# Window attention in a fused layer: sums taken with the values, copies in two buffers, a norm begun earlier

## The chip, the cores and the metric

The kernel runs on one core of one Trainium2 chip. The metric is the device time in microseconds (us) of one execution. Fourteen runs of the kernel before have a median of 957.48 us (954.87 to 962.13). The engines are called PE (TensorE: matmuls; PEld is its weight load), DVE (VectorE), ACT (ScalarE), POOL (GpSimd) and SP (SyncE, which issues most of the DMAs).

## The reference

The input is x of 4 x 128 x 64 x 64 (images, channels, rows, columns). Layer 0 norms each pixel over channels, adds a 3x3 depthwise convolution of that norm to it, cuts the image into windows of 16x16 pixels, and attends in each window over 5x5 neighbours, with 2 branches of 4 heads of 32 channels:

```python
y = _layernorm2d(x, ln_g, ln_b)
y = y + _cpe(y, cpe_w, cpe_b)              # 3x3, per channel
logits = jnp.einsum('nbhdij,nbhdkij->nbhkij', q, k_nb) * scale
attn = jax.nn.softmax(logits, axis=3)      # over the 25 neighbours
o = jnp.einsum('nbhkij,nbhdkij->nbhdij', attn, v_nb)
```

Neighbours outside the window are zeros, so each of them adds exp(0) = 1 to the softmax sum and nothing to the output. The heads' outputs are projected, the two branches added, and x added. Layer 1 treats the pixels as tokens: linear attention with a running sum over them (`_L1_attn_ref`), then a recurrence over all 4096 pixels of an image (`_L1_ffn_ref`).

## The kernel before

**Tiling.** A band is 16 rows of one image; there are 16 bands of 4 windows, 64 windows in all. The main loop (L684) goes window by window. For window i it issues:

- `logits` (L355): four masks and 24 products of 32 rows each, four heads side by side in the array, into four PSUM banks; then four exponentials on ACT (L376), each of 128x512, into `es0` to `es3`.
- `weighted` of the window before, i-1 (L379): the softmax sums `den` as four products of a column block of ones with the exponentials (L385), the values `ops` as 24 products (L397), both with 32 output rows per head, so that four heads work side by side. ACT copies both banks to SBUF (`den` L388, `o_sb` L405). A DMA lays the sums out as `dc`, 128 x 16; DVE adds the count of padded neighbours and inverts (L408 to L412); a DMA puts the result in DRAM (`rd`, L414) and another reads it back, one copy for each of 32 rows (`rden`, L416).
- `scaled` of window i-2 (L422): POOL multiplies `o_sb` by `rden` into the band's `oT` (L425).
- `window_inputs` of window i+1 (L315): the products q, k and v from `y2w`, the convolved pixels; each is copied out of PSUM by ACT (L330, L342). Two DMAs (L344, L345) make the middle block of keys out of halves of the two others.

**Gaps.** Between these pieces lie six gaps (`between`, L677). Each gap advances two generators by one step: `behind`, the layer-1 work of the band before (`layer1`, L593: 24 steps, begun in the second window of the next band), and `ahead`, which makes the pixels of the next band (`front`, L646: `norm_rows`, then `convolve` for each half). In the first window of a band `ahead` gets three gaps only (0, 4 and 5), otherwise six: 21 steps in a band. A half of the convolution is one ACT instruction and eight DVE instructions of 128x512 (L271, L273) and a copy to `y2w` on ACT (L309). In the layer-1 order, `output0` (L442) reads `oT` and gives the projected tokens, `measure`, `norm` and `turn` are the second layer norm, `keep` sends tokens to DRAM.

**Order.** `in_order` (L160) keeps PE, DVE, ACT and POOL in the program's order. SP isn't in that list: the order of its DMAs is chosen when the program is built. `p1`, `p2` and `p3` are pools of one, two and three buffers; PSUM is one pool of eight banks, handed out in turn (`bank`, L176). After the main loop a recurrence of 32 steps (L796 on) follows, which the change doesn't touch.

Names of the windows in what follows: a band's **first, second, third and fourth window** are those with i % 4 = 0, 1, 2, 3.

Of the kernel before, what the change touches and what calls it, by code (L numbers as in the profile page):

```python
# [46 lines left out]
def conv_attn_hybrid(ctx: ExitStack, tc: tile.TileContext, ins: dict, out: bass.AP):  # L47
# [101 lines left out]
    for i in range(2):  # L149
        t = const.tile([P, 4, P + 1], F32, name=f"v1_{i}")  # L150
        nc.vector.memset(t, 1.0)
        v1s.append(t)

    stats = const.tile([P, B * T // 512, 6], F32, name="stats")

    wx = const.tile([P, B, NH, SEG, HSEGS], F32, name="wx")
# [22 lines left out]
    def run(g):  # L179
        for _ in g:  # L180
            pass
# [42 lines left out]
    def norm_rows(n):  # L224

        b, wi = bands[n]
        y = padded(n)
        below = wi < NB - 1
        first, end = (0 if wi == 0 else 1), NCH + below

        def evict(dst, src):
            nc.scalar.activation(dst, src, AF.Identity, bias=ln_b, scale=ln_g)

        groups = [(0, 4), (4, 8), (8, 9)] if wi == 0 else [(1, 5), (5, end)]

        found, xn = {}, {}
        for g in range(len(groups) + 2):
            if g < len(groups):
                found[g] = measured(
                    [xin[n][:, j, :] if j < NCH else heads.pop(n + 1) for j in range(*groups[g])],  # L240
                    1e-6,
                )
            if g - 1 in found:
                xn[g - 1] = normed(found.pop(g - 1), p2, "xf")
            if g - 2 in xn:
                j0, j1 = groups[g - 2]
                rows = turned(xn.pop(g - 2), 0, j1 - j0)[:, : (j1 - j0) * P]
                rows = rows.rearrange("p (r w) -> p r w", w=W)
                k1 = min(2 * j1 + 1, WS + 2)
                evict(y[:, 2 * j0 + 1 : k1, 1 : W + 1], rows[:, : k1 - 2 * j0 - 1, :])  # L250
                if j1 > NCH:
                    evict(padded(n + 1)[:, 1:3, 1 : W + 1], rows[:, 2 * (NCH - j0) :, :])
            yield
        ks = slice(1, WS + 1 + below)
        nc.gpsimd.tensor_copy(y[:, ks, 0:1], y[:, ks, 1:2])
        nc.gpsimd.tensor_copy(y[:, ks, W + 1 :], y[:, ks, W : W + 1])

        if wi == 0:
            nc.gpsimd.tensor_copy(y[:, 0, :], y[:, 1, :])
        if below:  # L260
            nc.gpsimd.tensor_copy(padded(n + 1)[:, 0, :], y[:, WS, :])
        else:
            nc.gpsimd.tensor_copy(y[:, WS + 1, :], y[:, WS, :])
# [51 lines left out]
    def window_inputs(w, n, wj):  # L315
# [14 lines left out]
            nc.scalar.copy(w[name], pps)  # L330
            yield
        vps = bank()
        v_sb = p2.tile([P, 3, BR * P], F32, tag="v_sb", name="v_sb")
        for e in range(2):
            nc.tensor.matmul(  # L335
                vps[:, e * 256 : (e + 1) * 256],
# [2 lines left out]
                start=True,  # L339
                stop=True,  # L340
            )
        nc.scalar.copy(v_sb[:, 0::2, :], vps.rearrange("p (e t) -> p e t", e=2))  # L342

        nc.sync.dma_start(v_sb[:64, 1, :], v_sb[64:, 0, :])  # L344
        nc.sync.dma_start(v_sb[64:, 1, :], v_sb[:64, 2, :])  # L345
        w["v"] = v_sb
        yield

    pieces = [(br, n) for br in range(BR) for n in range(len(BLOCKS))]
# [5 lines left out]
    def logits(w):  # L355
# [16 lines left out]
                    stop=(br, n) == pieces[-1],  # L372
                )
        for h in range(HEADS):
            es = p2.tile([P, BR * WT], F32, tag=f"es{h}", name=f"es{h}")
            nc.scalar.activation(es, sps[h], AF.Exp, scale=scale)  # L376
            w["es", h] = es

    def weighted(w):  # L379


        ops, dps = bank(), bank()
        for h in range(HEADS):
            rows = slice(h * HD, (h + 1) * HD)
            nc.tensor.matmul(dps[rows], ones[:, :HD], w["es", h], start=True, stop=True)  # L385

        den = p1.tile([P, BR * WT], F32, tag="den", name="den")
        nc.scalar.copy(den, dps)  # L388
        dc = p2.tile([P, 16], F32, tag="dc", name="dc")
        nc.sync.dma_start(dc, den[::HD, :])  # L390
        yield
        for br, n in pieces:
            cols, _ = spans(br, n)
            for h in range(HEADS):
                rows = slice(h * HD, (h + 1) * HD)
                c0 = br * P + h * HD
                nc.tensor.matmul(  # L397
                    ops[rows, cols],
                    w["v"][:, n, c0 : c0 + HD],
                    w["es", h][:, cols],  # L400
                    start=(br, n) == pieces[0],
                    stop=(br, n) == pieces[-1],
                )
        o_sb = p1.tile([P, BR * WT], F32, tag="o_sb", name="o_sb")
        nc.scalar.copy(o_sb, ops)  # L405
        yield

        nc.vector.tensor_tensor(dc, dc, pad_c, ALU.add)  # L408
        rc = p2.tile([P, 16], F32, tag="rc", name="rc")
        nc.vector.reciprocal(rc, dc)  # L410
        nc.vector.tensor_tensor(dmax, dmax, dc, ALU.max)
        nc.vector.tensor_tensor(dmin, dmin, dc, ALU.min)  # L412
        rd = dram4.tile([HEADS, BR * WT], F32, tag="rd", name="rd")
        nc.sync.dma_start(rd.rearrange("h (a e) -> (h a) e", e=16), rc)  # L414
        rden = p1.tile([P, BR * WT], F32, tag="rden", name="rden")
        nc.sync.dma_start(rden, rd.unsqueeze(1).to_broadcast([HEADS, HD, BR * WT]))  # L416
        w["o"], w["rden"] = o_sb, rden
        yield

# [173 lines left out]
    def layer1(n, last):  # L593
# [2 lines left out]
        y, z = last  # L596
        order = [
            (keep, z), None,
            (norm, z), (product, y), None,
            (output0, a), (measure, a), None,  # L600
            (turn_last, z), None,
            (norm, a), (output0, c), (measure, c), None,
            (turn, a), None,
            (product, z), (norm, c), None,
            (queries, a), None,
# [40 lines left out]
    def front():  # L646


        for n in range(1, len(bands)):
            yield from norm_rows(n)  # L650
            if bands[n][1]:
                yield
            for half in range(2):
                yield from convolve(n, half)
                yield
            if n == 1:

                for _ in range(4):
                    yield


    nc.vector.tensor_scalar(cpe_w[:, 4:5], cpe_w[:, 4:5], 1.0, None, ALU.add)
# [9 lines left out]
    windows = {0: {}}  # L672
    run(window_inputs(windows[0], 0, 0))
    run(third)
    ahead, behind = front(), iter(())

    def between(i, gap):  # L677


        next(behind, None)  # L680
        if i < len(places) and (i == 0 or i % NB or gap in (0, 4, 5)):
            next(ahead, None)

    for i in range(len(places) + 2):  # L684
# [5 lines left out]
        if 2 <= i:  # L690
            m, wjm = places[i - 2]
            if wjm == NB - 1:
                run(behind)
                behind = layer1(m, halves.pop(m - 1, (None, None)))
        between(i, 0)
        if 2 <= i:
            scaled(m, wjm, windows.pop(i - 2))
        if i < len(places) and wj == 1 and n + 2 < len(bands):
            load(n + 2)
        sums = weighted(windows[i - 1]) if 1 <= i <= len(places) else iter(())  # L700
        for gap in (1, 2):
            next(sums, None)
            between(i, gap)
        run(sums)
        if i == 0:
            run(fourth)
        inputs = iter(())
        if i + 1 < len(places):
            windows[i + 1] = {}
            inputs = window_inputs(windows[i + 1], *places[i + 1])  # L710
        for gap in (3, 4, 5):
            next(inputs, None)
            between(i, gap)
        run(inputs)
    run(behind)
    run(layer1_end(*halves.pop(len(bands) - 1)))
    in_order()
# [782 lines left out]
```

## Time and profile before

| | us |
|---|---|
| median of 14 runs | 957.48 |
| the profiled execution's own time | 961.6 |
| its span, first to last instruction | 959.6 |
| PE busy | 884.9 (92%) |
| DVE busy | 747.8 (78%) |
| ACT busy | 542.3 (57%) |
| POOL busy | 263.5 (27%) |
| mean granted clock of PE | 0.972 |
| DMA, share of 16 engines, main queue | 19.1% |

Busy time is the time in which at least one instruction of the engine runs. A group's line gives its line in the kernel, engine and operation, what it writes and reads, its shape and count; then its busy time, the mean of one instruction in ns, and how long the engine was idle just before such an instruction, with what ended that idle time. Matmuls are pipelined and their ends are modelled, so starts of consecutive ones tell more than their lengths. A wait's line reads: who waited for whom, in total, how often, the longest. The span's sum is made against 959.6 us and the profiled time of 961.6, some 4 us above the median of the runs; a change in us is carried over to the median.

### The profile page before, as it was taken

The page shows a single profiled execution, that of the slowest core. Times are in us where ns is not written, and L with a number is a line of the kernel's source. Part 1 is how long each engine was busy: PE and PEld are TensorE (multiplying, and loading weights), DVE is VectorE, ACT ScalarE, POOL GpSimd, SP SyncE. Part 2 cuts the span into 40 slices and gives each one's busy share as a digit, 9 for nine tenths or more (in the row PEclk, how much of TensorE's full clock was granted, in tenths as well). Part 3 has the DMA queues.
Part 4 walks back from the last instruction along what each step waited for, and adds up shares of the span by engine and source line. Part 5 has one row for each costly group of instructions (what it writes and reads, how often), then busy time and mean ns, then how long its engine had stood idle before and what let it go on. Part 6 is the DMA issues. An engine that isn't in the chain of part 4 may idle for free.

```text
span 959.6 us, 26560 instructions
## 1 busy us (share of the span) xinstructions
PE 884.9 (92%) x10508; PEld 657.7 (69%) x10508; DVE 747.8 (78%) x2452; ACT 542.3 (57%) x1010; POOL 263.5 (27%) x359
## 2 busy tenths in 40 slices
PE   5979999999999999999999999999999999978784
PEld 3746676777777768677777767776767778655442
DVE  6345878888887878797888889787879887567786
ACT  3554656575656565665656565656556565522553
POOL 2013131413232231413131323223131312121185
PEclk9978999999999999999999999999999999988898
DMA  3112112121212111212112121111121111101853
GB/s 117 33 36 60 36 52 62 46 57 61 58 46 62 54 55 48 71 37 70 48 45 58 58 57 58 51 57 54 48 66 39 50 40 51 42 34 31 348 203 146
DMA packets 53045, 63.46 MB, mean 66 GB/s; under 512 B 22960, under 2 KB 33840, under 8 KB 52400
## 3 DMA queue, kind: packets, MB, share of 16 engines
q1 hardware_dynamic: 51184, 56.91, 19.1%
q10 hardware_dynamic: 1728, 4.77, 1.3%
q8 instruction: 85, 1.39, 0.6%
q14 instruction: 48, 0.39, 0.2%
HBM read 35.44 MB, written 17.30 MB: 55 GB/s over the span
## 4 chain that ended last, share of the span: by engine, by line
PE 70%; DMA 11%; DVE 7%; ACT 4%; POOL 4%; issue 2%; SPq 1%; ACTq 0%; POOLq 0%; DVEq 0%
PE bank L322 10%; PE bank L450 6%; PE bank L367 6%; DMA rden<-rd 6%; PE bank L212 6%; PE bank L397 5%; PE bank L385 5%; PE bank L335 5%; PE bank L479 5%; PE bank L558 3%; PE bank L587 3%; PE bank L539 3%; PE bank L522 3%; PE bank L560 3%; DMA res<-resd 2%; PE bank L496 2%
## 5 line engine op out<-in xcount | busy, mean ns | idle before, releaser
L273 DVE SCALAR_TENSOR_TENSOR y<-ypad,cpe_w,y 128x512 f32<-128x512 f32 x240 | 191.4, 798 | 14.2 <-ACT y L271 10.6
L425 POOL TENSOR_TENSOR oT<-o_sb,rden 128x512 f32<-128x512 f32 x64 | 85.6, 1337 | 365.0 <-DMA rden<-rd 311.1
L376 ACT ACTIVATE es<-bank 128x512 f32<-128x512 f32 x256 | 132.2, 602 | 76.2 <-PE bank L367 76.2
L196 POOL TENSOR_TENSOR rs<-rs,mhalf 128x4 f32<-128x4 f32 (+2 forms) x100 | 107.1, 1071 | 8.3
L367 PEld LDWEIGHTS bank<-q,k 32*128 32x128 f32 x3072 | 98.1, 189 | 9.7 <-ACT k L330 8.7
L367 PE MATMUL bank<-q,k 32*128 32x96 f32 (+1 forms) x3072 | 96.7, 271 | 7.8 <-ACT k L330 7.8
L195 POOL TENSOR_SCALAR rs<-mv 128x4 f32<-128x4 f32 (+2 forms) x100 | 25.1, 251 | 268.9 <-DVE mv L193 174.2
L203 DVE TENSOR_SCALAR xn<-x,mv,rs 128x128 f32<-128x128 f32 x256 | 81.2, 378 | 21.5 <-POOL rs L196 21.5
L405 ACT COPY o_sb<-bank 128x512 f32<-128x512 f32 x64 | 37.6, 587 | 75.0 <-POOL oT L425 57.1
L397 PEld LDWEIGHTS bank<-es,v_sb 128*32 128x32 f32 x3072 | 57.0, 110 | 30.9 <-issue 16.7
L450 PE MATMUL bank<-woT,oT 128*128 128x128 f32 x512 | 67.7, 288 | 5.1 <-POOL oT L425 5.1
L385 PE MATMUL bank<-es,ones 128*32 128x512 f32 x512 | 72.3, 639 | 0.0
L479 PE MATMUL bank<-xl,awT 128*128 128x512 f32 x128 | 70.1, 631 | 1.0 <-ACT xl L474 1.0
L450 PEld LDWEIGHTS bank<-woT,oT 128*128 128x128 f32 x512 | 64.4, 201 | 9.0 <-POOL oT L425 6.2
L397 PE MATMUL bank<-es,v_sb 128*32 128x96 f32 (+1 forms) x3072 | 70.2, 240 | 0.0
L322 PE MATMUL bank<-y2w,wqT 128*128 128x256 f32 x256 | 67.3, 386 | 1.0 <-DVE y2w L273 1.0
L322 PE MATMUL bank<-y2w,wkT 128*128 128x256 f32 x256 | 66.7, 384 | 0.0
L335 PE MATMUL bank<-wvT,y2w 128*128 128x256 f32 x256 | 66.4, 382 | 0.0
L342 ACT COPY v_sb<-bank 128x512 f32<-128x512 f32 x64 | 37.6, 588 | 50.3 <-PE bank L335 49.4
L330 ACT COPY q<-bank 128x512 f32<-128x512 f32 x64 | 37.8, 591 | 39.7 <-PE bank L322 39.3
L191 DVE BATCH_NORM_STATS2 st<-x 128x6 f32<-128x128 f32 x256 | 55.5, 279 | 1.1
L322 PEld LDWEIGHTS bank<-y2w,wqT 128*128 128x128 f32 x256 | 45.6, 193 | 13.0 <-issue 7.2
(124 smaller groups left out, 1734.8 us busy)
## 6 DMA issues: line engine op xcount, KB each, us to landing
rden<-rd SPq DMA_DIRECT2D x64, 256.0 KB
v_sb<-v_sb SPq DMA_DIRECT2D x128, 64.0 KB
resd<-rs_o SPq DMA_DIRECT2D x32, 256.0 KB
out<-ot SPq DMA_DIRECT2D x32, 256.0 KB
xin<-in_xt SPq DMA_DIRECT2D x15, 512.0 KB
res<-resd SPq DMA_DIRECT2D x2, 2048.0 KB
res<-resd ACTq DMA_DIRECT2D x2, 2048.0 KB
dc<-den SPq DMA_DIRECT2D x64, 8.0 KB
```

The costliest lines, as they stand in the source:

```text
L196: nc.gpsimd.tensor_tensor(rs[:, :n], rs[:, :n], mhalf[:, :n], ALU.pow)
L203: nc.vector.tensor_scalar(xn[:, j, :], piece, mv[:, j, 0:1], rs[:, j : j + 1], ALU.subtract, ALU.mult)
L273: nc.vector.scalar_tensor_tensor(y2, src, cpe_w[:, tap : tap + 1], y2, ALU.mult, ALU.add)
L322: nc.tensor.matmul(pps[:, br * WT : (br + 1) * WT], wT[:, br * P : (br + 1) * P], y2, start=True, stop=True,)
L335: nc.tensor.matmul(vps[:, e * 256 : (e + 1) * 256], y2[:, e * P : (e + 1) * P], wvT, start=True, stop=True,)
L367: nc.tensor.matmul(sps[h][:, cols], w["k"][rows, k0 : k0 + P], w["q"][rows, cols], start=False, stop=(br, n) == pieces[-1],)
L376: nc.scalar.activation(es, sps[h], AF.Exp, scale=scale)
L385: nc.tensor.matmul(dps[rows], ones[:, :HD], w["es", h], start=True, stop=True)
L397: nc.tensor.matmul(ops[rows, cols], w["v"][:, n, c0 : c0 + HD], w["es", h][:, cols], start=(br, n) == pieces[0], stop=(br, n) == pieces[-1],)
L425: nc.gpsimd.tensor_tensor(oTs[n][:, :, :, wj * WS : (wj + 1) * WS], w["o"].rearrange("p (a r c) -> p a r c", a=BR, c=WS), w["rden"].rearra ...
L450: nc.tensor.matmul(yps[:, j * P : (j + 1) * P], oT[:, br, t], woT[:, br, :], start=br == 0, stop=br == BR - 1,)
L479: nc.tensor.matmul(zps, awT[:, m * P : (m + 1) * P], h.xl, start=True, stop=True)
```

## The change

1. **Copied attention in two buffers.** `o_sb` moves from `p1` to `p2`; the exponentials `es0` to `es3` move from `p2` to `p1`; `den` goes away, `o_mid` (one buffer) comes.
2. **Order of the window.** `weighted` of window i now runs in window i itself, its two matmul parts ahead of gaps 3 and 4, and its last part (the inverse and its DMAs) after the next window's logits. `window_inputs` of i+1 moves forward: q ahead of gap 1, k ahead of gap 2, v ahead of gap 5 rather than ahead of gaps 3, 4 and 5. `scaled` runs for window i-1 ahead of v.
3. **Norm of the band ahead.** `norm_rows` is cut into single steps (measure, measure, scale, then turn with the next scale), and `ahead` gets the gaps 0, 2 and 4 of a band's first window. The empty steps are counted anew, so that the convolution keeps its place. In `layer1` the order of the first steps changes: `output0` and `measure` of the first half come second rather than third, and those of the other half fourth rather than fifth; `norm` of the first half then follows `measure` of the second.
4. **Values with ones beside them.** The v tile becomes `vts`: two constant tiles of 49 blocks of 32 columns, filled with ones once by POOL, into which every second block is written with values. One product now has 64 output columns, a head's values and a block of ones, so that it gives both the values and the sums; two heads go side by side, in two passes (heads 0 and 3 into `o_sb`, heads 1 and 2 into `o_mid`). The sums come out of three DMAs, and one more DMA moves the middle 64 rows from `o_mid` to `o_sb`.

The number of DVE, ACT and PE operations on other tiles is unchanged. The core of the diff:

```diff
+    vts = []
+    for i in range(2):
+        t = const.tile([P, 1 + 6 * BR * HEADS, HD], F32, name=f"vt{i}")
+        nc.gpsimd.memset(t, 1.0)
+        vts.append(t)
...
+        measure(0)
+        yield
+        measure(1)
+        yield
+        scale(0)
+        yield
+        for g in range(len(groups)):
+            turn(g)
+            scale(g + 1)
+            measure(g + 2)
             yield
...
-        nc.scalar.copy(v_sb[:, 0::2, :], vps.rearrange("p (e t) -> p e t", e=2))
-        nc.sync.dma_start(v_sb[:64, 1, :], v_sb[64:, 0, :])
-        nc.sync.dma_start(v_sb[64:, 1, :], v_sb[:64, 2, :])
+        low, mid, high = (slice(1 + 16 * k, 17 + 16 * k) for k in range(3))
+        nc.scalar.copy(
+            vt[:, 1:, :].rearrange("p (e k) d -> p e k d", e=3)[:, 0::2, 0::2],
+            vps.rearrange("p (e k d) -> p e k d", e=2, d=HD),
+        )
+        nc.sync.dma_start(vt[:64, mid, :], vt[64:, low, :])
+        nc.sync.dma_start(vt[64:, mid, :], vt[:64, high, :])
...
-            es = p2.tile([P, BR * WT], F32, tag=f"es{h}", name=f"es{h}")
+            es = p1.tile([P, BR * WT], F32, tag=f"es{h}", name=f"es{h}")
...
+    PAIRS = (((0, 0, True), (64, 3, False)), ((0, 1, False), (64, 2, True)))
...
-            nc.tensor.matmul(dps[rows], ones[:, :HD], w["es", h], start=True, stop=True)
-        den = p1.tile([P, BR * WT], F32, tag="den", name="den")
-        nc.scalar.copy(den, dps)
-        nc.sync.dma_start(dc, den[::HD, :])
...
+        o_sb = p2.tile([P, BR * WT], F32, tag="o_sb", name="o_sb")
+        o_mid = p1.tile([P, BR * WT], F32, tag="o_mid", name="o_mid")
+        for pair, o in zip(PAIRS, (o_sb, o_mid)):
+            ops = bank()
+            for br, n in pieces:
+                cols, _ = spans(br, n)
+                for r0, h, values_first in pair:
+                    k = 1 + 2 * ((n * BR + br) * HEADS + h) - (not values_first)
+                    nc.tensor.matmul(
+                        ops[r0 : r0 + 2 * HD, cols],
+                        w["v"][:, k : k + 2, :].rearrange("p i d -> p (i d)"),
+                        w["es", h][:, cols],
+                        start=(br, n) == pieces[0],
+                        stop=(br, n) == pieces[-1],
+                    )
+            nc.scalar.copy(o, ops)
+            if o is o_sb:
+                nc.sync.dma_start(dc[:HD], o[HD : HD + 1, :])
+                nc.sync.dma_start(dc[3 * HD :], o[2 * HD : 2 * HD + 1, :])
+            else:
+                nc.sync.dma_start(dc[HD : 3 * HD], o[0 : 3 * HD + 1 : 3 * HD, :])
+            yield
...
+        nc.sync.dma_start(o_sb[HD : 3 * HD], o_mid[HD : 3 * HD])
...
             (keep, z), None,
+            (output0, a), (measure, a), None,
             (norm, z), (product, y), None,
-            (output0, a), (measure, a), None,
-            (turn_last, z), None,
-            (norm, a), (output0, c), (measure, c), None,
+            (output0, c), (measure, c), None,
+            (turn_last, z), (norm, a), None,
...
-        if i < len(places) and (i == 0 or i % NB or gap in (0, 4, 5)):
+        if i < len(places) and (i == 0 or i % NB or gap in (0, 2, 4)):
...
+        run(sums)
+        inputs, sums = iter(()), iter(())
+        if i + 1 < len(places):
+            windows[i + 1] = {}
+            inputs = window_inputs(windows[i + 1], *places[i + 1])
+        if i < len(places):
+            sums = weighted(windows[i])
+        between(i, 0)
+        next(inputs, None)
+        between(i, 1)
+        next(inputs, None)
+        between(i, 2)
+        next(sums, None)
+        between(i, 3)
+        next(sums, None)
+        between(i, 4)
+        if 1 <= i <= len(places):
+            scaled(*places[i - 1], windows.pop(i - 1))
+        run(inputs)
+        between(i, 5)
```

## The prediction

> **What bounds the kernel now.** I read the page first, then the busy time of one band's windows, the groups by shape, the order of time in a fourth window, and stretches by granted clock. The page:
>
> ```profile
> PE 884.9 (92%) x10508; PEld 657.7 (69%) x10508; DVE 747.8 (78%) x2452; ACT 542.3 (57%) x1010; POOL 263.5 (27%) x359
> ```
>
> PE is the bound. The view of stretches, cut at the four logits of the band that starts at 371.2 us (columns: length, then busy time of PE, PEld, DVE, ACT, POOL):
>
> ```profile
> 371.20:384.27 13.07, 13.07 (x178) 11.25 (x178) 12.11 (x50) 7.14 (x14) 2.47 (x3) 1.00 0.19 55
> 384.27:400.25 15.98, 14.30 (x176) 11.12 (x176) 12.70 (x56) 9.03 (x17) 7.71 (x15) 1.00 0.15 47
> 400.25:411.85 11.60, 11.60 (x141) 7.39 (x140) 9.59 (x24) 8.08 (x15) 3.39 (x3) 1.00 0.32 82
> 411.85:423.28 11.43, 11.43 (x156) 8.63 (x157) 10.10 (x21) 7.54 (x14) 1.27 (x1) 1.00 0.14 39
> ```
>
> PE runs without a gap except in the second window (1.68 us lost). So a wait of ACT, POOL or DMA is worth something only where PE stands still, and each new PE wait costs its whole length. DVE is at 12.1 of 13.1 us in the first window, close behind. The groups by shape say where PE waits (last column) and what the attention's products take:
>
> ```profile
> L385 PE MATMUL bank<-es,ones 128*32 128x512 f32 x512 | 72.3, 639 | 0.0
> L397 PE MATMUL bank<-es,v_sb 128*32 128x96 f32 x2048 | 70.2, 250 | 0.0
> L539 PE MATMUL bank<-v,k 128*128 128x129 f32 x256 | 34.9, 278 | 4.4 <-ACT k L516 4.4
> L212 PE MATMUL bank<-ident,xf 128*128 128x128 f32 x128 | 30.9, 328 | 24.5 <-DVE xf L203 20.3 <-ACT es L376 4.1
> ```
>
> [...]
>
> ```profile
> 60.00:63.40 3.40, 1.94 (x47) 1.31 (x45) 0.55 (x4) 2.57 (x5) 0.16 (x1) 1.00 0.03 2
> 63.40:66.80 3.40, 3.40 (x56) 1.92 (x55) 0.00 (x0) 2.53 (x5) 0.00 (x0) 0.50 0.26 76
> 592.50:595.90 3.40, 2.11 (x40) 1.52 (x33) 3.40 (x22) 2.54 (x5) 2.31 (x5) 1.00 0.18 51
> 595.90:599.30 3.40, 3.40 (x12) 1.00 (x12) 2.88 (x8) 1.38 (x3) 2.77 (x4) 0.50 0.21 77
> 647.10:650.50 3.40, 2.11 (x20) 1.13 (x16) 2.57 (x18) 2.96 (x6) 2.53 (x4) 1.00 0.02 6
> 650.50:653.90 3.40, 3.40 (x62) 1.73 (x54) 3.33 (x9) 2.40 (x5) 1.27 (x2) 1.00 0.04 8
> ```
>
> After 1.94 busy of 3.40 the next stretch runs at half clock (0.50); after 2.11 once it does and once it doesn't. So about 1.3 us of idle inside one stretch is the border. Half a clock stretch cost 1.2 us where it struck: the second windows at 591.6 and 697.1 us have 15.65 and 15.63 us of PE busy, their neighbours 14.45. [...] the 48 narrow products of a window start within 0.85 us. [...] the trace has no load of 64.
>
> **The change, part by part.**
>
> *Values with ones.* Four heads side by side with 32 outputs become two with 64, in two passes. Before, a window takes 1.0 us for the sums (402.94 to the next start at 403.94) and 1.02 for the values (404.99 to 406.01). Each pass streams the same 512 columns as the values now, so two passes are 2.04 us against 2.02. Between starts, a set of 96 columns takes 82 ns, of 64 columns 56. Loads of 128 columns pace the logits at 1.53 us / 12 sets = 127 ns, those of 32 columns fit in 56; on the line between, 64 columns take 80 ns, an upper end. Then each of 8 sets of 64 columns in a window (those of 96 are longer anyway) would lose up to 24 ns: 0 to 0.19 us a window, 0 to 12 us in all. I take 5. ACT keeps two copies of 0.59 us. The v copy in blocks of 32 should cost the 0.59 to 0.62 us of the other rearranging copies (L309 in the trace: 0.62).
>
> *More DMAs.* Eight on SP's queue per window, not five, at about 0.57 us of issue: 4.6 of 11.4 us. The built order puts the three `dc`, `o_mid` and the two `vt` ahead of `rd` and `rden`. `rd` to `oT` done took 8.1 us at the end of the trace (842.1 to 850.15); begun about 3 us into a window it ends at 11, about that window's end. `output0` reads the last `oT` of a band some 4 us later: hidden, and if it were 5 us later still each band would pay about 1 us. Behind `oT` on POOL stand only the later reciprocal roots for the norms. POOL's two fills lie before its first root at 6.4 us, by the 0.21 us of its 128-wide fill 2.6 us each at most: hidden behind the first load.
>
> *Two buffers.* ACT's wait for POOL (57 us in the list of waits) goes, but PE paid for it only at L539: 4.4 us gained. One buffer of `es` waits for the same window's values, a whole window earlier: nothing.
>
> *Norm begun earlier.* `xf` is scaled at gap 4 instead of gap 5, with both measurements done. The wait at L212 goes: 24.5 less about 8 at the very start is 16.2 us, and with it the two half-clock stretches, 2.4. The first norm of all has its last piece scaled after the other eight: 1.2 us more at the start.
>
> *Order of the window: the new wait.* In the built order PE's list of a fourth window is now logits, `scores`, then the q product of the next band's first half. This reads `y2w`, which ACT copies in the same gap 0, behind the four exponentials. The order of time before, in a fourth window:
>
> ```profile
> 412.08 1.48 PE L367 MATMUL bank<-q,k 32*128 32x96 f32 x48
> 413.49 1.16 PE L522 MATMUL bank<-f,f 128*128 128x128 f32 x8
> 413.59 2.07 ACT L376 ACTIVATE es<-bank 128x512 f32<-128x512 f32 x4 [0.94 <-PE bank L367]
> 414.58 1.07 PE L385 MATMUL bank<-es,ones 128*32 128x512 f32 x8
> 415.79 0.62 ACT L309 COPY y2w<-y 128x512 f32<-128x512 f32 x1
> ```
>
> Before, the sums and other work filled the time until gap 2. Now PE is done with `scores` at 414.58, and `y2w` is there at 416.41 in this band; in seven of the fifteen fourth windows that have the copy it is there 4.30 us after the window's start, that is 1.57 us after `scores`. The DVE work ahead of the last tap is 0.7 us less in the new order (the `dc` operations), so I take 1.6 us, fourteen times (the band after the first has spare steps and copies earlier): 22.4 us. It can't be hidden: everything on PE stands behind it. A gap of 1.6 us falls with 1.3 us or more into one clock stretch in (3.41 - 1.6 + 0.6) / 3.41 = 0.7 of positions: 9 of 14, at 1.2 us: 10.8 us.
>
> *DVE in the first window.* Both measurements (1.2 and 1.0 us) and `xf` (1.1 to 2.2) now come before DVE's last part of `attend`, for which `keep` on PE waits. Before, `x` was there at 385.38 and `keep` began at 385.90: 0.5 us to spare, against 2 to 3 us more work and 1 to 2 us of lag saved by the stall above: -0.5 to 1.5 us. In the second window `norm` of the first half now stands behind `measure` of the second: 0 to 1 us at `turn`. I take 0.45 for both, 13 times: 6.
>
> *Start and end.* Band 0's windows lost 4.9, 1.5, 1.4 and 1.8 us at 52 to 80 us (starts of L367 and L450), because POOL's first `oT` waited 13.9 us for `rden` and held back ACT and the q and k copies. In the new order the first convolution's inputs are ready before, and only the wait of `output0` for the fourth `oT` stays, some 4 to 5 us: 6 gained. At the end `oT` came 12.7 us after the last but one window's start; now about 10.8: 2 gained.
>
> **The sum** against the profiled 961.6 us. Gone: 16.2 + 4.4 + 2.4 + 6 + 2 = 31.0. Added: 22.4 + 10.8 + 5 + 6 + 1.2 = 45.4. That is +14.4: 976.0 there, **972** on the scale of the median.
>
> **The rivals.**
>
> *The clock holds and the rest hides (faster).* If no half-clock stretch follows the new wait and loads, DVE lag and `turn` cost nothing, only 22.4 + 1.2 are added: 31.0 - 23.6 = 7.4 less, 950. For it: after 1.3 us of idle only two of nine such waits in the steady part were followed by half clock. Against: at 60 and 70 us waits of 1.4 to 1.5 us were, each time. It decides at 7.4 us: more than six half-clock stretches alone turn it. 0.17.
>
> *The narrow passes bind (slower still).* If loads of two tiles don't overlap as those of four do, [...] Against: four 32-column loads fit in 56 ns, the same number of columns. 0.06.
>
> *The change doesn't do it: the wait at L212 stays*, because DVE, with the same work as before, is as late at gap 4: 16.2 + 2.4 not gained, about 990. Against: between gap 4 and the turn lie v, a step of layer 1, and logits, 4 us. 0.07.
>
> *Both waits nearly balance*, at 1.2 us with three half-clock stretches: within 0.2%. 0.07.
>
> **How the numbers follow.** The likeliest case has 0.63, with its own range of 962 to 986 (half-clock stretches 3 to 14, loads 0 to 12, DVE and `turn` 0 to 15). The range of 950 to 990 takes in the faster case and the lost norm. 0.2% (1.9 us) is about what a measurement of this kernel can tell from no change. Slower by more: 0.63 + 0.06 + 0.07 = 0.76; same 0.07; faster 0.17.
>
> **What would show it.** In the profile after: PE idle of about 22 us at the q product, released by ACT's `y2w`, 14 times; none at L212 for `xf` in the steady part; granted clock of PE below 0.972; the values' starts 2.0 to 2.2 us a window; fourth windows of about 13 us or more, second windows near 14.3. The prediction is wrong if the q product doesn't wait, if the fourth windows stay at full clock, or if `output0` waits for `oT` in each band.

## The result

| | before | after |
|---|---|---|
| median, us | 958.76 (47 runs) | 976.92 (10 runs, 974.99 to 981.3) |
| ratio after / before | | 1.0195, 95% interval 1.0176 to 1.0214 |
| the profiled execution's own time, us | 961.6 | 977.3 |
| its span, us | 959.6 | 975.6 |
| mean granted clock of PE | 0.972 | 0.978 |

The changed kernel is 1.9% slower, on the predicted side and within the range: 976.9 us, where 972 was predicted. By spans it is 16.0 us longer where the sum gave 14.4. But the terms of that sum are only partly right: two are far off, in opposite directions.

### The profile page after: what moved, and what is told of

It reads as the page before. It is cut to its first block, busy times and chain, and to the rows that moved or that the text cites. A ratio compares the mean times of both kernels' runs of the same rounds, so it can differ in the third digit from the quotient of the medians.

```text
span 975.6 us, 26069 instructions
## 1 busy us (share of the span) xinstructions
PE 889.5 (91%) x9996; PEld 711.5 (73%) x9996; DVE 756.4 (78%) x2452; ACT 544.7 (56%) x1010; POOL 251.1 (26%) x361
## 4 chain that ended last, share of the span: by engine, by line
PE 63%; DVE 20%; DMA 7%; ACT 4%; issue 3%; POOL 1%; SPq 0%; ACTq 0%; DVEq 0%; POOLq 0%
PE bank L421 11%; PE bank L344 9%; PE bank L219 7%; DVE y L295 7%; PE bank L480 6%; PE bank L393 6%; PE bank L509 5%; PE bank L357 4%; PE bank L526 3%; PE bank L617 3%; DMA res<-resd 2%; ACT es L402 2%; DVE st L198 2%; DVE state L577 2%; PE bank L588 2%
## 5 line engine op out<-in xcount | busy, mean ns | idle before, releaser
L295 DVE SCALAR_TENSOR_TENSOR y<-ypad,cpe_w,y 128x512 f32<-128x512 f32 x240 | 210.6, 878 | 13.1 <-ACT y L293 9.1
L455 POOL TENSOR_TENSOR oT<-o_sb,rden 128x512 f32<-128x512 f32 x64 | 85.6, 1337 | 324.7 <-DMA rden<-rd 299.8
L421 PEld LDWEIGHTS bank<-es,vt 128*64 128x64 f32 x3072 | 120.5, 138 | 40.8 <-ACT k L352 16.7
L421 PE MATMUL bank<-es,vt 128*64 128x96 f32 (+1 forms) x3072 | 145.1, 243 | 5.1 <-DMA vt<-vt 5.1
L202 POOL TENSOR_SCALAR rs<-mv 128x4 f32<-128x4 f32 (+2 forms) x100 | 19.5, 195 | 332.3 <-DVE mv L200 172.6
L203 POOL TENSOR_TENSOR rs<-rs,mhalf 128x4 f32<-128x4 f32 (+2 forms) x100 | 99.4, 994 | 8.3
L344 PE MATMUL bank<-y2w,wqT 128*128 128x256 f32 x256 | 68.6, 391 | 24.3 <-ACT y2w L331 23.2
L428 ACT COPY o_mid<-bank 128x512 f32<-128x512 f32 x64 | 37.5, 585 | 74.7 <-PE bank L421 72.2
L344 PEld LDWEIGHTS bank<-y2w,wqT 128*128 128x128 f32 x256 | 44.9, 191 | 38.3 <-ACT y2w L331 25.9
L365 ACT COPY vt<-bank 128x512 f32<-128x512 f32 x64 | 37.5, 587 | 61.7 <-PE bank L357 60.4
L344 PE MATMUL bank<-y2w,wkT 128*128 128x256 f32 x256 | 66.8, 384 | 0.0
L513 DVE TENSOR_SCALAR low<-low 128x512 f32<-128x512 f32 x64 | 26.9, 421 | 45.9 <-ACT low L511 45.9
L344 PEld LDWEIGHTS bank<-y2w,wkT 128*128 128x128 f32 x256 | 47.3, 194 | 18.2 <-issue 10.8
L487 DVE TENSOR_TENSOR x<-bank,xin 128x512 f32<-128x512 f32 x32 | 22.1, 691 | 49.0 <-PE bank L480 49.0
```

The lines of the kernel that those rows point to most:

```text
L203: nc.gpsimd.tensor_tensor(rs[:, :n], rs[:, :n], mhalf[:, :n], ALU.pow)
L295: nc.vector.scalar_tensor_tensor(y2, src, cpe_w[:, tap : tap + 1], y2, ALU.mult, ALU.add)
L344: nc.tensor.matmul(pps[:, br * WT : (br + 1) * WT], wT[:, br * P : (br + 1) * P], y2, start=True, stop=True,)
L421: nc.tensor.matmul(ops[r0 : r0 + 2 * HD, cols], w["v"][:, k : k + 2, :].rearrange("p i d -> p (i d)"), w["es", h][:, cols], start=(br, n) ...
L455: nc.gpsimd.tensor_tensor(oTs[n][:, :, :, wj * WS : (wj + 1) * WS], w["o"].rearrange("p (a r c) -> p a r c", a=BR, c=WS), w["rden"].rearra ...
```

## The profile after

Each kernel's span is cut in three: up to the first logits of the third band (the ninth window), the thirteen bands from there, and the rest. The table gives the mean length of the four windows of a band over these thirteen bands, cut where PE starts a window's masks, and below it the three parts of the span. The first two columns say where the 16.0 us came from; the others belong to the experiments. A half-clock stretch is one of 3.41 us in which PE was granted half of its clock (0.50): in the traces of both kernels any two changes of the granted clock lie a whole number of 3.41 us apart (before, at half clock: 63.41 to 66.82, 73.65 to 77.06, 595.89 to 599.30, 701.70 to 705.11).

| us | before | after | q, k late | norm alone | old sums | small product | gaps 1, 3, 4 | two buffers | late, old sums | inputs early | norm, buffers |
|---|---|---|---|---|---|---|---|---|---|---|---|
| first | 13.00 | 14.25 | 13.22 | 13.49 | 14.09 | 13.23 | 13.09 | 13.00 | 13.22 | 13.34 | 13.88 |
| second | 15.73 | 13.86 | 13.86 | 13.46 | 13.82 | 13.86 | 14.72 | 15.74 | 13.82 | 18.02 | 13.46 |
| third | 11.60 | 11.83 | 11.83 | 11.60 | 11.76 | 11.83 | 11.83 | 11.60 | 11.76 | 11.73 | 11.60 |
| fourth | 11.64 | 13.38 | 11.95 | 11.71 | 14.01 | 13.20 | 13.64 | 11.20 | 11.90 | 14.91 | 11.20 |
| two bands ahead | 112.9 | 112.5 | 110.9 | 113.4 | 106.1 | 111.6 | 111.9 | 102.8 | 106.2 | 115.4 | 107.0 |
| thirteen bands | 675.7 | 693.1 | 661.2 | 653.4 | 697.7 | 677.6 | 692.6 | 670.1 | 659.0 | 754.0 | 652.0 |
| rest | 171.0 | 170.0 | 167.6 | 169.9 | 166.0 | 166.0 | 165.7 | 170.7 | 164.5 | 171.7 | 170.4 |
| half-clock stretches in the bands after the first two | 2 | 1 | 0 | 0 | 6 | 0 | 3 | 2 | 0 | 19 | 0 |

After against before: -0.4, +17.4 and -1.0 us. Inside a band the second window won 1.87 us, and the first (+1.25), third (+0.23) and fourth (+1.74) lost 3.22.

The page of the changed kernel:

```profile
PE 889.5 (91%) x9996; PEld 711.5 (73%) x9996; DVE 756.4 (78%) x2452; ACT 544.7 (56%) x1010; POOL 251.1 (26%) x361
```

PE is busy only 4.6 us longer than before, in a span 16.0 us longer: the rest is new standing still. DVE is busy 8.6 us longer for the same 2452 instructions, which a count of instructions could not foresee. One band of the changed kernel in the view of stretches (length, then busy time of PE, PEld, DVE, ACT, POOL, then granted clock):

```profile
219.05:233.46 14.41, 13.84 (x169) 12.09 (x169) 13.75 (x58) 7.43 (x14) 4.85 (x7) 1.00 0.25 76
233.46:247.25 13.79, 13.79 (x167) 11.73 (x166) 10.68 (x51) 8.87 (x16) 4.25 (x9) 1.00 0.34 96
247.25:258.88 11.63, 11.63 (x134) 8.33 (x134) 9.65 (x19) 7.77 (x14) 2.75 (x3) 1.00 0.24 68
258.88:272.08 13.20, 11.58 (x148) 9.70 (x148) 10.12 (x19) 7.70 (x14) 1.28 (x1) 1.00 0.19 53
```

PE stands still in the fourth window (13.20 less 11.58) instead of the second, and in the first DVE works 13.75 of 14.41 us. The groups of PE by shape:

```profile
L421 PE MATMUL bank<-es,vt 128*64 128x96 f32 x2048 | 144.5, 254 | 0.0
L421 PE MATMUL bank<-es,vt 128*64 128x64 f32 x1024 | 74.0, 222 | 5.1 <-DMA vt<-vt 5.1
L344 PE MATMUL bank<-y2w,wqT 128*128 128x256 f32 x256 | 68.6, 391 | 24.3 <-ACT y2w L331 23.2 <-DVE y2w L295 1.1
L219 PE MATMUL bank<-ident,x 128*128 128x128 f32 x128 | 25.8, 293 | 8.3 <-DVE x L602 8.3
L219 PE MATMUL bank<-ident,xf 128*128 128x128 f32 x128 | 22.1, 293 | 9.9 <-DVE xf L210 9.3
```

The norm's wait for `xf`, 24.5 us before, is down to 9.9, all of it ahead of the first band; L539's successor, L569, has no wait left. In their place stand 23.2 us at the q product (L344), 8.3 at the transposes of `keep` (L219 for `x`), and 5.1 at the values, for the two DMAs that build `vt`. The order of time at the start of a fourth window:

```profile
258.89 1.53 PEld L393 LDWEIGHTS bank<-q,k 32*128 32x128 f32 x48
...
260.51 1.16 PE L552 MATMUL bank<-f,f 128*128 128x128 f32 x8
260.67 2.06 ACT L402 ACTIVATE es<-bank 128x512 f32<-128x512 f32 x4 [1.00 <-PE bank L393]
...
262.60 0.64 ACT L331 COPY y2w<-y 128x512 f32<-128x512 f32 x1
263.29 0.73 PEld L344 LDWEIGHTS bank<-y2w,wqT 128*128 128x128 f32 x4 [1.81 <-ACT y2w L331]
263.29 1.13 PE L344 MATMUL bank<-y2w,wqT 128*128 128x256 f32 x4 [1.62 <-ACT y2w L331]
```

PE has finished `scores` at 261.67 and stands until 263.29, because ACT copies `y2w` behind the four exponentials.

## The experiments

The first theory was the prediction's: q's early place makes a wait worth some 22 us and more, the earlier norm is a gain, and the values with ones cost little. The rival was that what matters is the DVE or the order as a whole, so that moving q back would give back far less than it costs.

### q and k late again

```diff
+        late = i < len(places) and i > 3 and wj == NB - 1
         between(i, 0)
-        next(inputs, None)
+        if not late:
+            next(inputs, None)
         between(i, 1)
-        next(inputs, None)
+        if not late:
+            next(inputs, None)
         between(i, 2)
+        if late:
+            next(inputs, None)
         next(sums, None)
         between(i, 3)
+        if late:
+            next(inputs, None)
         next(sums, None)
```

> The changed kernel, but in the fourth window of each band from the second band on, q is issued ahead of gap 3 and k ahead of gap 4 rather than ahead of gaps 1 and 2. Theory (PE waits at the q product for ACT's y2w, 14 times 1.62 us): the q product comes after scores, a feature product and a turn, some 1.5 us later, so 0 to 0.3 us of each wait is left; fourth windows 11.6 us instead of 13.2; 976.9 - 21 = 956 us. Rival (DVE's lag sets the pace of fourth and first windows together, the wait at q only hides it): the first windows grow by what the fourth ones lose, to 15 us or more, and the time stays above 970.

Measured: 938.73 us, 0.9784 of before (0.9745 to 0.9822). That is 38 us faster than the changed kernel, 17 below the theory and some 20 more than the fall of the wait itself. The list of waits, PE at q (total, times, longest):

```profile
PE bank L344 <- ACT y2w L331: 5.0, 14, 0.9
```

23.2 has become 5.0. But the table shows a second gain that nobody moved: the first windows go from 14.25 to 13.22. While PE stands still in a fourth window, DVE gets fewer inputs and work of its own moves into the next first window. In the changed kernel DVE is busy for 10.12 of 13.20 us in the fourth window shown above (19 instructions), and the first window after it is

```profile
272.08:286.59 14.51, 13.72 (x169) 12.06 (x169) 13.85 (x58) 7.43 (x14) 4.88 (x7) 1.00 0.25 75
```

and in the version with late q a fourth and a first window are

```profile
251.88:263.79 11.91, 11.59 (x147) 9.39 (x147) 10.32 (x23) 7.60 (x14) 1.28 (x1) 1.00 0.22 58
263.79:276.98 13.19, 13.19 (x169) 12.00 (x168) 12.67 (x55) 7.22 (x14) 4.88 (x7) 1.00 0.28 83
```

DVE has 19 instructions in the fourth window with the stall and 23 without it, though that window is shorter, and 58 and 55 in the first. So a stall of PE in one window made a stall in the next. That is shown for the pair of windows; which single DVE instruction carries it over isn't. Moved work may not be all of it: the version with a small product on POOL, below, finds a second cause.

### The norm alone

The kernel before, with the third part of the change only.

```diff
-        if i < len(places) and (i == 0 or i % NB or gap in (0, 4, 5)):
+        if i < len(places) and (i == 0 or i % NB or gap in (0, 2, 4)):
```

and the cut of `norm_rows` into single steps as in the changed kernel.

> The kernel before with one part of the change alone: the norm of the band ahead in single steps at gaps 0, 2 and 4 of a first window. Theory (the wait for xf in second windows goes, nothing else moves): 16.2 us of waits and two half-clock stretches go, second windows 13.9 us instead of 15.7, 958.8 - 18 = 941 us. Rival (measure at gap 0 stands ahead of DVE's part of attend, so PE waits for x at keep in the first window, as in the changed kernel): first windows grow by 0.5 to 1.3 us and only 2 to 10 us are gained.

Measured: 939.1 us, 0.9791 (0.9743 to 0.984), as the theory has it, though the first windows do grow by the 0.5 us of the rival. The second windows fall by 2.27 us, the first rise by 0.49, and both half-clock stretches go. The part is worth 20 us; in the changed kernel that is paid back elsewhere.

### The sums as before

The changed kernel, with four products of ones for the sums and four heads side by side for the values, `v_sb` and `den` as before.

```diff
-        for pair, o in zip(PAIRS, (o_sb, o_mid)):
...
+        for h in range(HEADS):
+            rows = slice(h * HD, (h + 1) * HD)
+            nc.tensor.matmul(dps[rows], ones[:, :HD], w["es", h], start=True, stop=True)
...
+                nc.tensor.matmul(
+                    ops[rows, cols],
+                    w["v"][:, n, c0 : c0 + HD],
+                    w["es", h][:, cols],
...
```

> The changed kernel with the sums and values as before (two products sets of 32 columns, four heads side by side, v tile of 3 x 256, one DMA for the sums, no o_mid), in the new order. Theory (the narrow passes cost little: 1.04 us of start to start against 1.00 and 1.02): 976.9 - 4 = 973 us, each first part 1.00 us. Rival (the loads of 64 columns or the added DMAs cost more, hidden in other rows): 965 us or less.

Measured: 969.72 us, 1.0114 (1.0058 to 1.017), 7 us faster than the changed kernel and between theory and rival. It isn't the passes: second and third windows differ by 0.04 and 0.07 us. The gain lies in the first two bands, 106.1 against 112.5 us. In the changed kernel PE waits there for the DMAs that make the middle keys' values, which have twice the bytes (128 KB each, 64 KB in this version) and more DMAs ahead of them on SP's queue (eight a window there, five here); from the list of waits:

```profile
PE bank L421 <- DMA vt<-vt: 5.1, 3, 2.6
```

(The part after the thirteen bands, 166.0 against 170.0, is no evidence: it is as short in two versions that keep the new sums.) This version has the same wait at q, yet six half-clock stretches instead of one, which hides part of its gain: the four fourth windows with one such stretch and a wait of 1.61 us take 14.82 us instead of 13.12, 1.7 us more each. The clock can be read there by itself. Two pairs of stretches of this version, cut at the 3.41 us of the clock's changes:

```profile
252.99:256.41 3.42, 1.81 (x33) 1.52 (x29) 2.82 (x9) 2.56 (x5) 0.00 (x0) 1.00 0.17 38
256.41:259.82 3.41, 3.41 (x6) 2.07 (x7) 0.00 (x0) 0.58 (x1) 0.00 (x0) 0.50 0.11 37
362.22:365.63 3.41, 1.80 (x12) 1.51 (x11) 2.24 (x7) 2.39 (x5) 0.00 (x0) 1.00 0.05 7
365.63:369.05 3.42, 3.42 (x20) 1.78 (x19) 1.60 (x3) 2.93 (x5) 0.00 (x0) 1.00 0.20 69
```

PE is busy for 1.8 us in both first stretches, and only one is followed by half clock. In the changed kernel seven waits at q of 1.62 us lie wholly inside one stretch: the one that begins 1.45 us into it (793.47 us) was followed by half clock, the six that begin after 0.16 to 0.71 us were not. Together with this version and the one with gaps 1, 3 and 4 below there are, from 100 us on, 24 such waits. The six that begin 1.45 us or later were all followed by half clock; the eighteen that begin at 1.22 us or before, never. So for this wait, in these three runs, the outcome went with its place. Place alone doesn't tell it: a wait of 1.57 us at the transposes of `xf`, in the version with early inputs (below), began only 0.56 us into its stretch, PE was busy there for 1.85 us, and half clock followed:

```profile
130.32:133.74 3.42, 1.85 (x11) 1.30 (x12) 2.75 (x18) 2.79 (x6) 2.51 (x5) 1.00 0.19 69
133.74:137.15 3.41, 3.41 (x12) 1.01 (x11) 2.82 (x7) 1.57 (x3) 1.37 (x2) 0.50 0.20 75
```

What decides is not shown: PE's busy time is the same 1.8 us, but at q a late wait has the narrow products of the logits in the stretch ahead of it (33 instructions of PE in the first stretch above), an early one the wide products of q after it (12).

### A small product on POOL

DVE's 8.6 us more on the same instructions asked for a cause. Its convolution steps (L295) last 878 ns on average, 798 before. From the order of time of the changed kernel, at the end of a fourth window (the second line is two steps back to back, of 1.71 and 0.75 us):

```profile
269.24 1.28 POOL L455 TENSOR_TENSOR oT<-o_sb,rden 128x512 f32<-128x512 f32 x1 [11.48 <-DMA rden<-rd]
269.36 2.50 DVE L295 SCALAR_TENSOR_TENSOR y<-ypad,cpe_w,y 128x512 f32<-128x512 f32 x2
```

A step takes 0.75 us elsewhere. Of these two, the first lies beside POOL's product and takes 1.71; the second begins at 271.1, after the product's end, and takes 0.75. A convolution step reads `ypad` and `y`, both in SBUF. The product lies beside the first step for 1.16 us (269.36 to 270.52), and that step takes 1.0 us more than 0.75. In the changed kernel 42 steps begin while such a product runs: all take over 1 us (1.03 to 1.74), and no other step does. The 20 in which the product begins only during the step keep 0.74 to 0.75 us. In the kernel before 17 begin while a product runs: 15 take over 1 us, two 0.98. The step `f` (L514), the same operation and shape but with one of its inputs in PSUM, lies beside it ten times and keeps its 750 ns. Why the two differ is not shown by the traces. The new theory: the convolution's steps now begin beside a running product more often, 42 times against 17, and that costs the first windows. The next version leaves POOL's place and its waits as they are and cuts the product to 2 of the 16 rows of each window; the other rows of `oT` are a constant, so its output is not the attention's.

```diff
-            oTs[n][:, :, :, wj * WS : (wj + 1) * WS],
+            oTs[n][:, :, 0:2, wj * WS : (wj + 1) * WS],
-            w["o"].rearrange("p (a r c) -> p a r c", a=BR, c=WS),
+            w["o"].rearrange("p (a r c) -> p a r c", a=BR, c=WS)[:, :, 0:2],
...
```

> The changed kernel with POOL multiplying only 2 of 16 rows of each window (the other rows of oT are a constant 1, so the projection works on numbers that are not the attention's). Theory (POOL's 1.28 us product slows the DVE instructions that run beside it, 42 of 240 convolution steps at up to 1.7 us instead of 0.75, and so DVE reaches attend late in first windows): convolution steps at 0.75 us on average, PE's wait at keep nearly gone, first windows 13.3 us instead of 14.25, 976.9 - 12 = 965 us. Rival (the order of DVE's work alone, with measure ahead of attend, makes it late): the steps get shorter but the first windows stay within 0.3 us and the time within 3 us.

Measured: 957.24 us, 0.9993 (0.9973 to 1.0013): 19.7 us faster than the changed kernel, 8 more than the theory. The groups of DVE and of POOL in the changed kernel, then in this version:

```profile
L295 DVE SCALAR_TENSOR_TENSOR y<-ypad,cpe_w,y 128x512 f32<-128x512 f32 x240 | 210.6, 878 | 13.1 <-ACT y L293 9.1
L210 DVE TENSOR_SCALAR xn<-x,mv,rs 128x128 f32<-128x128 f32 x256 | 81.8, 382 | 1.4 <-POOL rs L203 1.4
L514 DVE SCALAR_TENSOR_TENSOR f<-bank,ab,low 128x512 f32<-128x512 f32 x64 | 48.0, 750 | 2.3
L455 POOL TENSOR_TENSOR oT<-o_sb,rden 128x512 f32<-128x512 f32 x64 | 85.6, 1337 | 324.7 <-DMA rden<-rd 299.8 <-ACT k L352 20.3 <-issue 3.6
```

```profile
L298 DVE SCALAR_TENSOR_TENSOR y<-ypad,cpe_w,y 128x512 f32<-128x512 f32 x240 | 180.0, 750 | 13.8 <-ACT y L296 9.7
L213 DVE TENSOR_SCALAR xn<-x,mv,rs 128x128 f32<-128x128 f32 x256 | 70.5, 341 | 1.4 <-POOL rs L206 1.4
L457 POOL TENSOR_TENSOR oT<-o_sb,rden 128x64 f32<-128x64 f32 x64 | 25.8, 403 | 346.9 <-DMA rden<-rd 287.3 <-ACT o_sb L431 37.9 <-ACT o_mid L431 13.2
```

With the product cut from 1337 to 403 ns the 240 steps take 750 ns on average, where the changed kernel's take 878, with 42 of them over 1 us (15 before). The scalings `xn` of the second norm, which read one 128x128 tile in SBUF, fall as well, from 382 to 341 ns; in the changed kernel those beside the product average 830 ns, the others 336. First windows fall to 13.23, the same as with late q; the wait at q stays (22.6 us). So the first windows' loss needs both the stall at q and the long product: either one removed brings back 1.0 us a band. The two are linked. Late q, with the product as long as ever, leaves only 6 of the 16 long steps in fourth windows (the 26 in third windows stay), while the kernel before has 14 there, no stall, and first windows of 13.00. How much of the loss is work moved by the stall and how much is steps lengthened isn't separated.

### The norm one gap later

```diff
-        if i < len(places) and (i == 0 or i % NB or gap in (0, 2, 4)):
+        if i < len(places) and (i == 0 or i % NB or gap in (1, 3, 4)):
```

> The changed kernel, but the norm of the band ahead takes the gaps 1, 3 and 4 of a first window rather than 0, 2 and 4, so that DVE's first measurement of the next band stands behind both first parts of attend. Theory (DVE reaches attend late, for its order as much as for the slow convolution steps): PE's wait at keep (8.3 us in all, and the stretched transposes beside it) goes, first windows 13.3 us instead of 14.25, the q wait stays at 14 times 1.62; 976.9 - 12 = 965 us. Rival (only POOL's product makes DVE late): first windows stay above 14 us and the time within 3 us of 977.

Measured: 972.68 us, 1.0126 (1.0082 to 1.0171), between theory and rival. The first windows fall by 1.16 us, as the theory has it, but the second rise by 0.86. In the order of time, at the start of a second window:

```profile
235.50 0.59 PE L219 MATMUL bank<-ident,x 128*128 128x128 f32 x2 [0.77 <-DVE x L602]
```

It is the same wait, of the transposes of `keep` for `x` (7.4 us in all, 8.3 in the changed kernel), one window later: moved, not removed. Three half-clock stretches took a part of the rest.

### Two buffers alone

The kernel before, with one letter changed.

```diff
-        o_sb = p1.tile([P, BR * WT], F32, tag="o_sb", name="o_sb")
+        o_sb = p2.tile([P, BR * WT], F32, tag="o_sb", name="o_sb")
```

> The kernel before with o_sb in two buffers and nothing else. Theory (PE pays for ACT's wait for POOL only at accumulate): the 4.4 us at L539 go, fourth windows 11.2 to 11.4 us each, and some of the waits in the first band; 959 - 5 = 954 us. Rival (ACT's 57 us of waiting is hidden wholly): within 2 us of 959.

Measured: 944.91 us, 0.9817 (0.9795 to 0.984): 16 us faster, beyond both. The fourth windows fall by 0.44 (L539's wait is gone), 5.6 us over the thirteen bands; ten more come in the first two bands. In the kernel before, in the fourth window of band 0:

```profile
49.41 0.59 ACT L405 COPY o_sb<-bank 128x512 f32<-128x512 f32 x1 [4.51 <-POOL oT L425]
```

and with two buffers

```profile
44.16 0.65 ACT L405 COPY o_sb<-bank 128x512 f32<-128x512 f32 x1
```

The kernel keeps ACT in the program's order (`in_order`), and q and k of the next window stand behind this copy. While the pipeline fills, POOL hasn't freed the one buffer, because it waits 13.9 us for its own input, `rden`; so PE loses 4.92 us in that window. From its start to the third band the kernel before takes 65.9 us, with two buffers 56.5.

### The inputs early, and nothing else

The kernel before, with q, k and v ahead of gaps 1, 2 and 5 from the second band on.

```diff
+        early = i > 3
         for gap in (1, 2):
+            if early:
+                next(inputs, None)
             next(sums, None)
```

> The kernel before with q, k and v ahead of gaps 1, 2 and 5 from the second band on, and nothing else of the change. Theory (the place of q alone makes the wait): PE waits 14 times 1.6 us for ACT's y2w, fourth windows 12.9 us instead of 11.6, second windows keep their wait for xf; 959 + 23 = 982 us. Rival (the wait needs the other parts too, for the sums' place or DVE's order): less than 10 us slower.

Measured: 1046.19 us, 1.0886 (1.0857 to 1.0914): far beyond both.

```profile
PE bank L322 <- ACT y2w L309: 30.2, 14, 2.4
PE bank L212 <- DVE xf L203: 28.1, 12, 8.1
PE bank L212 <- DVE xn L203: 15.2, 19, 2.5
```

The wait at q is there without any other part of the change, a little longer than in it. With it came what the sum did not hold: later `xf`, so that second windows have 2.5 us of waits instead of 1.3, and 19 half-clock stretches; PE's mean granted clock is 0.948 (0.972 before). In the kernel before, then, the early place of q and k costs 85 us, almost three times the wait at q itself.

### The best of both, twice

First late q and k together with the old sums (the edits of the first and third experiment):

> The changed kernel with q and k late in fourth windows and with the sums and values as before: both repairs at once. Theory (the two costs add up, 38 and 7 us): 976.9 - 45 = 932 us, the first band without waits for v, fourth windows 11.9 us. Rival (the 7 us of the old sums were the half-clock stretches' or the first windows', already gone): 938 us.

Measured: 933.71 us, 0.971 (0.969 to 0.9731), 28 us faster than the kernel before and close to the theory: these two gains add up. Then the kernel before with the norm and the second buffer (the edits of the second and sixth):

> The kernel before with two parts of the change: the norm of the band ahead begun in the gaps 0, 2 and 4 of a band's first window, and `o_sb` in two buffers. Order of the window and sums stay as before. Theory (the two act at different places: the norm takes away the wait at L212 in the second windows, the buffer the waits at L539 in the fourth windows and some ten us in the first two bands): alone they gave 939.1 and 944.9, some 20 and 16 us, so both together about 924 us. Rival (the waits of the first two bands, which the norm alone left at L465, L554 and L382, have one cause for both, or the freed time is lost at the next wait): 932 us or more, no better than the 933.7 of the changed kernel with late q and k and the old sums.

Measured: 930.99 us, 0.9761 (0.9709 to 0.9814), its kernel before having 952.57 in that comparison. The two intervals overlap, and which is better isn't told. The gains of norm and buffer do not add up: by spans 22.9 and 16.1 alone, 30.2 together, so the time is 7 us above the theory and 1 under the rival's bound. Part of even this may be the other chip on which this comparison was made: in it the gain is 21.6 us, in that of the norm alone it was 20.0, so by the medians the buffer's share beside the norm is not shown. The fourth windows are at 11.20, but the first rise from 13.49 with the norm alone to 13.88, with DVE busy for 13.01 of 13.71 us in this band:

```profile
207.46:221.17 13.71, 13.68 (x177) 11.24 (x177) 13.01 (x59) 7.42 (x14) 4.84 (x7) 1.00 0.18 55
```

That fits a first window which DVE limits, so that time saved ahead of it is handed back there; no experiment here tests it.

## Why the prediction was right, and where not

**The wait at q (22.4) was right in place, cause and size.** 14 waits, 23.2 us, most of them 1.62 us; 1.6 was taken.

**L212 (16.2 + 2.4) was right.** No wait for `xf` is left in the thirteen bands and both half-clock stretches went. The second windows won 24.3 us in all; part of that is work moved into the first.

**Half clock at the fourth windows (10.8) failed.** The step that puts 1.3 us or more of the gap into one clock stretch in 0.7 of positions was right: by the trace it was ten of fourteen (0.7 of fourteen is ten as well; the sum has nine). But only one of these was followed by half clock, and PE's mean granted clock rose to 0.978 where less than 0.972 was expected. The prediction's own sign, "if the fourth windows stay at full clock", says the same. What failed is the step before it, "So about 1.3 us of idle inside one stretch is the border": at 1.62 us the waits went both ways. The price of 1.2 us was too low besides. The fourth window that was struck, below one that wasn't:

```profile
738.51:751.71 13.20, 11.58 (x147) 9.70 (x147) 9.53 (x20) 7.70 (x14) 1.36 (x1) 1.00 0.19 52
790.67:805.56 14.89, 13.27 (x147) 10.58 (x146) 10.15 (x21) 7.69 (x14) 1.81 (x1) 0.89 0.17 47
```

That is 1.7 us, half of a stretch: ten such stretches would have cost 17 us. The same waits in the version with old sums were struck six times. This term hangs on where the waits fall, and from one kernel to the next that can't be told: 0 to 6 in the versions with this wait and the earlier norm.

**DVE in the first window (6) was mis-sized: 13.** The prediction looked for the order of DVE's instructions and had `keep` late behind the measurements, as it is. But it left out that POOL's product lengthens some of them, and it counted the stall as a help. The runs show 14.25 us against 13.22 or 13.23 as soon as either the stall at q or POOL's long product is away: 1.02 in each of thirteen bands. The step had "1 to 2 us of lag saved by the stall above"; taking the stall away gave 1.0 us a band back instead.

**Values with ones (5) was right about the passes.** By starts each takes 1.04 us (226.67 to 227.71, 228.80 to 229.84), 2.08 in place of 2.02. But "More DMAs", costed as hidden, looked only at the way from `rd` to `oT`, and the DMAs of `vt` were not hidden in the first two bands: 5.1 us at `vt`, 6.4 by the version with the old sums. The rival of narrow passes rested on loads of two heads that don't overlap; the trace, with 1.04 us a pass, doesn't show them.

**Two buffers (4.4) was right for L539 and missed the start.** The step for the start (6) saw that POOL held back ACT's copies there, but expected the cure from the new order; the buffer alone brings it, ten us large. In the changed kernel the DMAs of `vt` (5.1 us) and 3.0 us at `output0` take most of it away again: the start gained 0.4.

**Not foreseen:** 0.83 us at layer 1's `product` (L617, for `xl` on ACT) in every fourth band, 2.5 us in all, in third windows.

The wait at q and the norm were foreseen with their causes. That the total came out so close is luck: an overestimate (half clock, 9.1 too much) met underestimates (DVE 7, start 4, the third windows 2.5), with the second windows' larger gain against them. The rival of a faster kernel had the clock right, which mostly held, and fell because DVE was not hidden.

## What to carry to other kernels

Before moving a product forward in an engine's queue, look at the last engine that makes its input: here q's product went ahead to an input that ACT copies behind four exponentials, and the early place of q and k cost 38 us of the changed kernel. A stall can cost more than the time lost where it is seen, because it shifts the work of an engine near its limit into the next window. So measure each part of a change alone, and don't count on gains to add up: late q and old sums did, norm and buffer did not. And look at a single buffer first in the bands in which the pipeline fills.

## What the runs showed of the hardware

- A convolution step on DVE, with both inputs in SBUF, that begins while a 128x512 product runs on POOL (1.34 us on average) takes longer: 1.03 to 1.74 us in 42 of 42 in the changed kernel, 0.98 to 1.76 in 17 of 17 before, against 750 ns alone. The 20 steps of the changed kernel in which the product begins during the step keep 0.74 to 0.75 us. The scalings `xn` go from 336 to 830 ns on average beside it. The step `f`, with an input in PSUM, stays at 750 in 10 of 10. With the product at 403 ns the convolution steps take 750 ns on average, against 878.
- PE's clock after a wait at q of 1.62 us inside one stretch of 3.41 us: in the changed kernel half after the one that began at 1.45 us, full after the six that began at 0.16 to 0.71 us. With the versions with old sums and with gaps 1, 3 and 4: half in 6 of 6 that began at 1.45 us or later, full in 18 of 18 that began at 1.22 us or earlier, at the same 1.8 us of busy time. A wait of 1.57 us elsewhere, begun at 0.56 us, was followed by half clock. So were the four waits of 1.82 to 2.49 us that lie wholly inside one stretch in the two kernels (78.48 and 879.41 us before, 867.72 and 891.92 us after).
- A half-clock stretch in a window that PE limits cost 1.7 us (14.89 against 13.20 in the changed kernel, 14.82 against 13.12 with old sums).
- Two tiles of 64 output columns took 1.04 us for 512 columns, four of 32 took 1.0 to 1.02.
